# Layer 0's attention heads of images 1 to 3 written as one sequence with the bias computed five blocks ahead

## The chip, the cores and the metric

The kernel runs on one core of a Trainium2 chip. The metric is the device time of one execution in microseconds. The core has five engines with a queue each: TensorE (PE in the profile; its weight loads are PEld), VectorE (DVE), ScalarE (ACT), GpSimd (POOL) and SyncE (SP, which here issues DMAs). Each queue holds a fixed list of instructions and works it in order; an instruction that waits holds up everything behind it in its own queue. Matmul results go to PSUM, of which the kernel has two tiles of two banks ("big") and four of one bank ("bank").

## The reference, cut to what matters

Four layers follow each other on a batch of four images of 32 x 32 positions and 384 channels, each with a residual sum. The change is in the first, a deformable attention with 6 heads of 64 channels. Of it, what the changed code computes:

```python
attn = jnp.einsum('bmhc,bnhc->bhmn', qh, k) * scale
disp = (ref.reshape(1, n, 1, 2) - pos.reshape(Bq * G, 1, n, 2)) * 0.5
...
bias = _bilinear_sample(rpe_img, disp)          # one position table for each head
...
attn = jax.nn.softmax(attn + bias, axis=-1)
out = jnp.einsum('bhmn,bnhc->bmhc', attn, v).reshape(Bq, Hq, Wq, NC)
```

For each head, 1024 queries attend to 1024 sampled keys. To each logit a bias is added that is sampled bilinearly from a table, at a place that depends on the key's sampled position and on the query.

## The kernel before, in words

All data is float32. The program has two lanes of work. The front is layer 0 of an image; the trunk is layers 1 to 3 of an image. Image 0's front runs almost alone (`heads0`, ordered by hand, untouched by the change). After that, `Net.layer3` steps through the trunk of image b and, between its steps, through the front of image b+1: each generator yields the weight of the work it has just written, and the front is kept 0.1 of an image ahead. So the program text of trunk and front is interleaved. A planner then orders each engine's queue at build time: an instruction written earlier has the better rank, one that is not ready in the planner's reckoning is passed by one that is, and tiles of a tag share a fixed number of buffers. An edge without a semaphore (`add_manual_dep` with class NoSync) only forces one instruction behind another in a queue.

The heads of images 1 to 3 are written in `Front.layer0`: for each head h and each half q of the queries (16 rows, 512 queries) it calls `head0(h, q)`, a half-head; there are 12 of them in an image. Keys lie on the partitions, in eight blocks j of 128; queries lie on the free axis. A half-head does:

- **Bias and logits**, for each block: a gather by GpSimd (L830) fetches for each key a window of 17 rows of the table into `win` (4 buffers); ScalarE scales the upper rows into `z` (L842; 3 buffers) and VectorE adds the lower rows times their weight (L843); ScalarE scales the left columns into `lg` (L847; 13 buffers) and VectorE adds the right columns (L848). These four are one block's bias steps. Then TensorE multiplies keys and queries (L851), VectorE adds the product to the bias (L852) and keeps the running maximum over the blocks in `rmax` (L855, L857).
- **Maximum chain**: TensorE transposes `rmax` (L864), VectorE reduces it to one maximum for each query (`top`, L868), GpSimd puts the maxima on a diagonal (`diag`, L870), TensorE multiplies that with ones (L872), so that every partition has every query's maximum, and ScalarE copies it out of PSUM (`tb`, L876).
- **Softmax and values**, for each block: VectorE subtracts `tb` (L883), ScalarE takes the exponential (L884), TensorE accumulates values (`va`) and sums (`ones`) into one PSUM tile `po` (L886). At the end ScalarE copies the values over the queries in `qpad` (L890) and the sums into a row of the first `lg` tile (L893), and SP sends that row to `den` in DRAM (L894).

After every second head, `over_sums(k)` (L1112 to L1132) fetches the sums of two heads, inverts them (L1118), sends them to `rden` (L1121), loads them back, spread over the partitions, into two tiles of the tag `lg` (L1126) and multiplies `qpad` with them (L1131). `load_keys(h)` (SP) puts head h's keys into one of two padded tiles `kz`, one head ahead.

In the trunk, the longest stretch that runs beside the heads is layer 1's `pair`: TensorE's L1514, L1544, L1539, L1486 and L1381, ScalarE's exponentials L1522 and L1390 and its copies L1556, VectorE's L1551, L1389, L1477, L1480 and (at a pair's start) L1445, GpSimd's L1497 (`sg`).

## Time and profile before

| | us |
|---|---|
| median of 3 runs | 4557.96 (4557.15 to 4560.0) |
| the profiled execution | 4561.78 |
| its span, first to last instruction | 4560.0 |
| mean granted TensorE clock | 0.943 |

The profile is of one execution. Its page gives busy times of each engine, the granted TensorE clock (1.00 is full speed), and groups of instructions by source line, each with the idle time of the engine just before it and what ended that idle time (the releaser). Some groups on the changed lines, from the same profile:

| line | engine, what | count | mean ns |
|---|---|---|---|
| L830 | GpSimd, gather of `win` | 288 | 1122 |
| L842 / L847 | ScalarE, bias rows / columns | 288 each | 736 / 717 |
| L843 / L848 | VectorE, bias rows / columns | 288 each | 763 / 777 |
| L852 / L857 | VectorE, logit sum / running maximum | 288 / 216 | 684 / 688 |
| L868 | VectorE, reduction to `top` | 36 | 690 |
| L870 | GpSimd, diagonal | 36 | 1165 |
| L876 | ScalarE, copy to `tb` | 36 | 584 |
| L883 / L884 | VectorE subtraction / ScalarE exponential | 288 each | 701 / 628 |

The busy time of TensorE can hide slack, since its matmuls are pipelined and their ends are modelled; its idle time and the granted clock can be read off more surely.

### The profile page before, as it was taken

How to read it: one execution, taken by the hardware profiler on the slowest of the kernel's cores; microseconds unless marked ns; L12 is line 12 of the kernel's file. 1: busy time of each engine (PE TensorE's matmuls, PEld its weight loads, DVE VectorE, ACT ScalarE, POOL GpSimd, SP SyncE). 2: the span in 40 equal slices, each digit the busy share in tenths (PEclk: the TensorE clock that was granted, in tenths of full speed). 3: DMA queues.
4: the chain of work that ended last, by engine and by line, in shares of the span. 5: the costliest groups of instructions: out<-in, count | busy, mean ns of one | idle time of the engine just before them, and what ended most of it. 6: DMA issues, size and time to landing. Idle time of an engine off the chain costs nothing.

```text
span 4560.0 us, 47383 instructions
## 1 busy us (share of the span) xinstructions
PE 4131.4 (91%) x15896; PEld 1776.3 (39%) x15896; DVE 3135.2 (69%) x5909; ACT 2302.7 (50%) x3633; POOL 970.7 (21%) x978
## 2 busy tenths in 40 slices
PE   5699889999999898999999989799999998999998
PEld 2333334333334453433333444343333335344444
DVE  4599456878887627678878753667787874566654
ACT  2266334666664313556766332356566641466632
POOL 1644123212121103311212010422121211000000
PEclk8799899999999888999999989899999998999998
DMA  6444234222221244422322124532122213311011
GB/s 140 150 143 131 74 115 127 83 55 73 60 63 58 81 117 137 115 57 55 85 55 77 41 87 121 164 94 60 39 79 55 77 38 114 120 29 37 23 40 42
DMA packets 235924, 377.30 MB, mean 83 GB/s; under 512 B 117763, under 2 KB 167264, under 8 KB 235680
## 3 DMA queue, kind: packets, MB, share of 16 engines
q1 hardware_dynamic: 183640, 207.55, 16.2%
q0 software_dynamic: 39936, 145.53, 11.0%
q10 hardware_dynamic: 12104, 21.19, 1.4%
q8 instruction: 126, 2.06, 0.2%
q14 instruction: 118, 0.97, 0.1%
HBM read 294.19 MB, written 80.27 MB: 82 GB/s over the span
## 4 chain that ended last, share of the span: by engine, by line
PE 56%; DVE 15%; issue 7%; ACT 6%; DMA 3%; POOL 1%; another core or an unknown queue 0%; SPq 0%; ACTq 0%; DVEq 0%; POOLq 0%
PE bank L1544 13%; PE big L1514 5%; PE big L403 4%; PE bank L886 4%; PE bank L417 4%; PE big L1381 4%; PE bank L851 4%; PE bank L1486 3%; PE bank L1539 3%; DVE nmax L1389 2%; ACT big L1390 2%; PE bank L1219 2%; DVE e L1551 2%; PE big L666 2%; PE big L1684 1%
## 5 line engine op out<-in xcount | busy, mean ns | idle before, releaser
L1544 PE MATMUL bank<-whole,sg 128*128 128x512 f32 (+3 forms) x2304 | 847.0, 501 | 2.6 <-POOL sg L1497 2.6
L1551 DVE SCALAR_TENSOR_TENSOR e<-bank,gam,e 128x512 f32<-128x512 f32 x768 | 560.7, 748 | 316.2 <-PE bank L1544 177.3
L1390 ACT ACTIVATE big<-big,nmax 128x1024 f32<-128x1024 f32 x384 | 417.7, 1088 | 283.3 <-DVE nmax L1389 262.2
L1522 ACT ACTIVATE e<-big 128x1024 f32<-128x1024 f32 x384 | 381.1, 1020 | 328.2 <-PE big L1514 321.2
L1544 PEld LDWEIGHTS bank<-whole,sg 128*128 128x128 f32 x2304 | 399.4, 196 | 351.5 <-issue 259.4
L1389 DVE TENSOR_REDUCE nmax<-big 128x1 f32<-128x1024 f32 x384 | 453.2, 1219 | 84.6 <-PE big L1381 53.5
L830 POOL DMA_INDIRECT win<-strips,widx x288 | 323.2, 1122 | 703.3 <-DVE z L843 350.7
L1514 PE MATMUL big<-qa,ka 64*128 64x512 f32 x1536 | 432.8, 643 | 24.6 <-ACT big L1390 23.6
L1497 POOL TENSOR_SCALAR sg<-whole,gam 128x512 f32<-128x512 f32 x192 | 145.9, 760 | 1327.0 <-PE bank L1544 1064.5
L1381 PE MATMUL big<-k,q 32*128 32x512 f32 x1536 | 287.9, 662 | 43.2 <-ACT big L1390 26.0
L738 POOL DMA_INDIRECT gat<-pairs,sidx x192 | 206.2, 1074 | 412.9 <-DVE ix_gt L519 227.4
L851 PE MATMUL bank<-qpad,kz 128*128 128x512 f32 x576 | 280.6, 616 | 8.9 <-ACT gn L1556 8.3
L886 PE MATMUL bank<-lg,va 128*64 128x512 f32 x576 | 267.7, 609 | 21.4 <-ACT lg L884 21.3
L886 PE MATMUL bank<-lg,ones 128*64 128x512 f32 x576 | 267.0, 609 | 0.0
L848 DVE SCALAR_TENSOR_TENSOR lg<-z,bias_f,lg 128x512 f32<-128x512 f32 x288 | 220.0, 777 | 58.3 <-ACT lg L847 55.4
L1514 PEld LDWEIGHTS big<-qa,ka 64*128 64x128 f32 x1536 | 138.4, 190 | 280.1 <-issue 125.5
L1486 PE MATMUL bank<-e,vs 128*32 128x512 f32 x1536 | 231.1, 620 | 8.6 <-DVE vs L1480 8.4
L842 ACT ACTIVATE z<-win,bias_f 128x528 f32<-128x528 f32 x288 | 204.1, 736 | 42.2 <-DVE lg L848 22.2
L843 DVE SCALAR_TENSOR_TENSOR z<-win,bias_f,z 128x528 f32<-128x528 f32 x288 | 214.5, 763 | 8.5 <-issue 4.3
L883 DVE TENSOR_TENSOR lg<-lg,tb 128x512 f32<-128x512 f32 x288 | 187.0, 701 | 47.6 <-ACT tb L876 47.6
L852 DVE TENSOR_TENSOR lg<-bank,lg 128x512 f32<-128x512 f32 x288 | 192.2, 684 | 31.3 <-PE bank L851 30.6
L847 ACT ACTIVATE lg<-z,bias_f 128x512 f32<-128x512 f32 x288 | 201.5, 717 | 13.4 <-PE bank L886 5.7
(312 smaller groups left out, 6582.8 us busy)
## 6 DMA issues: line engine op xcount, KB each, us to landing
pairs<-xn SPq DMA_DIRECT2D x64, 192.0 KB
q<-qd SPq DMA_DIRECT2D x48, 256.0 KB
xg<-xgd SPq DMA_DIRECT2D x48, 256.0 KB
w<-in_gmat SPq DMA_DIRECT2D x16, 576.0 KB
w<-in_w_off SPq DMA_DIRECT2D x12, 576.0 KB
w<-in_Wqkv SPq DMA_DIRECT2D x12, 576.0 KB
a<-in_x SPq DMA_DIRECT2D x16, 384.0 KB
x<-a ACTq DMA_DIRECT2D x4, 1536.0 KB
```

The costliest lines, as they stand in the source:

```text
L830: nc.gpsimd.indirect_dma_start(out=win, out_offset=None, in_=self.strips[:, :], in_offset=bass.IndirectOffsetOnAxis(ap=self.widx[:, q, c : ...
L848: v.scalar_tensor_tensor(lg, z[:, :, 1 : HW + 1], sc(0, 0), lg, ALU.mult, ALU.add)
L851: nc.tensor.matmul(ps, kz[:, j * P : (j + 1) * P], both, start=True, stop=True)
L886: nc.tensor.matmul(po[out, :], w, lf, start=j == 0, stop=j == NJ - 1)
L1381: nc.tensor.matmul(ps[r][:, h * 512 : (h + 1) * 512], self.q4[rows, i * P : (i + 1) * P], self.k4[rows, 0:512], start=True, stop=True,)
L1389: v.tensor_reduce(nmax[:, r, i : i + 1], ps[r], AX.X, ALU.max, negate=True)
L1390: nc.scalar.activation(ps[r], ps[r], AF.Exp, bias=nmax[:, r, i : i + 1], accum_out=den[:, r, i : i + 1],)
L1486: nc.tensor.matmul(av[r0 : r0 + HD1, :], vs[:, r, :], es[h][:, r, :], start=j == 0, stop=j == NJ - 1,)
L1514: nc.tensor.matmul(ps[:, r, :], ka[rows, j * P : (j + 1) * P], qa[rows, cols], start=True, stop=True,)
L1522: nc.scalar.activation(e, ps, AF.Exp)
L1544: last = nc.tensor.matmul(ps[:, (mid - i0) * P :], sg[:, r, m, :], sim[:, h, r, m, (mid - i0) * P :], start=m == 0, stop=m == 1,)
L1551: v.scalar_tensor_tensor(e[:, r, :], ps, self.gam[:, 1:2], e[:, r, :], ALU.add, ALU.mult, accum_out=tot[:, r, h : h + 1],)
```

## The change

`head0` is gone; `Front.layer0` calls one generator `heads1` for the whole image. It numbers the 96 blocks (head, half, block) in one sequence. A call `bias()` writes the row steps of the next block and the column steps of the one before it; the row steps first issue the gather of the block two further on. Five calls stand ahead of the first logit. Each half-head then has eight more: after the logits of blocks 1, 3 and 5, between the transposes and the reduction to `top`, between the ones-matmul and the copy to `tb`, and after the softmax of blocks 1, 4 and 7. So at the start of each half-head the bias of its first five blocks is written already, across heads and across `over_sums`. `chain` puts an edge without a semaphore from each head instruction on VectorE, and likewise on ScalarE, to the one written before it on that engine (the two copies at the end of a half-head, `over_sums` and the trunk are outside). The sums now go out of PSUM into a row of `tb`. The yields are split anew (2.5 for each logit block, 2 after the reduction, 2 after the copy, 1.375 for each softmax block, 3 at the end); their sum for a half-head stays 38. The numbers of buffers stay.

```diff
             with self.scope("l0b"):
-                self.load_keys(0)
-                for h in range(G):
-                    if h + 1 < G:
-                        self.load_keys(h + 1)
-                    for q in range(2):
-                        yield from self.head0(h, q)
-                    if h % 2:
-                        yield from self.over_sums(h // 2)
+                yield from self.heads1()
...
+        def chain(ins):
+            engine = ins.ins.engine
+            if engine in last:
+                self.tc.add_manual_dep(
+                    ins.ins,
+                    last[engine],
+                    mybir.DependencyInfo(
+                        mybir.DependencyClass.NoSync, mybir.DependencyReason.DATA
+                    ),
+                )
+            last[engine] = ins.ins.name
...
+        def rows_of(i):
+            gather(i + 2)
+            if i < n:
+                wv = win.pop(i).rearrange("p (r c) -> p r c", c=WROW)
+                z[i] = self.wt([P, HH, HW + 1], "z", 3)
+                chain(nc.scalar.activation(
+                    z[i], wv[:, 0:HH, 0 : HW + 1], AF.Copy, scale=sc(i, 1, 1)
+                ))
+                chain(v.scalar_tensor_tensor(
+                    z[i], wv[:, 1 : HH + 1, 0 : HW + 1], sc(i, 1, 0), z[i], ALU.mult, ALU.add
+                ))
+
+        def cols_of(i):
+            if i < n:
+                zi = z.pop(i)
+                lg[i] = self.wt([P, HN], "lg", 13)
+                out = lg[i].rearrange("p (y x) -> p y x", x=HW)
+                chain(nc.scalar.activation(out, zi[:, :, 0:HW], AF.Copy, scale=sc(i, 0, 1)))
+                chain(v.scalar_tensor_tensor(
+                    out, zi[:, :, 1 : HW + 1], sc(i, 0, 0), out, ALU.mult, ALU.add
+                ))
+
+        todo = iter(range(n))
+
+        def bias():
+            i = next(todo, n)
+            rows_of(i + 1)
+            cols_of(i)
+
+        self.load_keys(0)
+        gather(0)
+        gather(1)
+        rows_of(0)
+        for _ in range(5):
+            bias()
+        for h in range(G):
+            if h + 1 < G:
+                self.load_keys(h + 1)
...
+            for q in range(2):
+                first = (2 * h + q) * NJ
...
+                for j in range(NJ):
+                    lf = lg[first + j]
+                    ps = self.bank()
+                    nc.tensor.matmul(
+                        ps, self.kz[h % 2][:, j * P : (j + 1) * P], both, start=True, stop=True
+                    )
+                    chain(v.tensor_tensor(lf, ps, lf, ALU.add))
+                    if j:
+                        chain(v.tensor_tensor(rmax, lg[first] if j == 1 else rmax, lf, ALU.max))
+                    if j % 2 and j < 6:
+                        bias()
+                    yield 2.5
+
+                ps = self.bank()
+                for i in range(NI):
+                    nc.tensor.transpose(
+                        ps[:, i * P : (i + 1) * P], rmax[:, i * P : (i + 1) * P], self.ident
+                    )
+                top = self.wt([P, NI], "top", 2)
+                bias()
+                chain(v.tensor_reduce(top, ps.rearrange("p (i n) -> p i n", i=NI), AX.X, ALU.max))
                 yield 2
...
+                tb = self.wt([P, HN], "tb", 2)
+                bias()
+                chain(nc.scalar.copy(tb, ps))
+                yield 2
+
+                po = self.bank()
+                for j in range(NJ):
+                    lf = lg.pop(first + j)
+                    chain(v.tensor_tensor(lf, lf, tb, ALU.subtract))
+                    chain(nc.scalar.activation(lf, lf, AF.Exp))
...
+                    if j % 3 == 1:
+                        bias()
+                    yield 1.375
...
+                den = tb[o0 : o0 + 1, :]
+                nc.scalar.copy(den, po[o0 : o0 + 1, :])
+                nc.sync.dma_start(self.den[h][:, q * HN : (q + 1) * HN], den)
+                yield 3
+            if h % 2:
+                yield from self.over_sums(h // 2)
```

## The prediction

> **What bounds the kernel.** I read the page's busy shares first, then its chain of waits, then the stretches in which the heads of images 1 to 3 run.
>
> ```profile
> span 4560.0 us, 47383 instructions
> PE 4131.4 (91%) x15896; PEld 1776.3 (39%) x15896; DVE 3135.2 (69%) x5909; ACT 2302.7 (50%) x3633; POOL 970.7 (21%) x978
> PE 56%; DVE 15%; issue 7%; ACT 6%; DMA 3%; POOL 1%; another core or an unknown queue 0%; SPq 0%; ACTq 0%; DVEq 0%; POOLq 0%
> L886 PE MATMUL bank<-lg,va 128*64 128x512 f32 x576 | 267.7, 609 | 21.4 <-ACT lg L884 21.3
> ```
>
> TensorE is the bound and the change takes no matmul away, so it can only win or lose TensorE's idle time and what goes with it, the granted clock. The heads' queue order matters where they run: by the starts of L842 and L886, 785 to 1560, 1905 to 2660 and 3018 to 3765 us. The busy time by stretch (columns: stretch, its length, busy PE, PEld, DVE, ACT, POOL, granted clock, DMA share, GB/s):
>
> ```profile
> 1270.30:1325.10 54.80, 54.64 (x232) 21.78 (x232) 39.32 (x79) 29.64 (x51) 3.82 (x5) 1.00 0.07 16
> 1325.10:1387.70 62.60, 56.35 (x211) 22.87 (x207) 59.21 (x121) 50.15 (x78) 27.32 (x24) 0.92 0.39 116
> 1079.70:1151.20 71.50, 63.11 (x228) 23.46 (x229) 67.34 (x122) 54.95 (x88) 28.20 (x26) 0.93 0.41 116
> 833.60:1509.80 676.20, 635.41 (x2526) 254.26 (x2526) 543.07 (x1060) 407.81 (x645) 128.66 (x129) 0.97 0.22 60
> 1949.30:2625.80 676.50, 636.16 (x2525) 255.09 (x2525) 542.35 (x1059) 407.89 (x645) 129.01 (x129) 0.97 0.21 60
> 3062.50:3739.00 676.50, 637.17 (x2526) 255.45 (x2526) 542.31 (x1059) 407.74 (x645) 128.29 (x129) 0.97 0.21 60
> ```
>
> The last three rows are one image's heads each, from the first logit sum (L852) to the last. TensorE idles 40.8, 40.3 and 39.3 us there (length less PE), 120.5 in all. The first row is one half-head with TensorE idle for 0.2 us; the second is the next, with 6.3 us idle, VectorE full (59.2 of 62.6) and the clock at 0.92. So the idle time is bunched. Why there? VectorE and ScalarE shortly before the third row, and SP's queue:
>
> ```profile
> 1068.82 0.75 DVE L1551 SCALAR_TENSOR_TENSOR e<-bank,gam,e 128x512 f32<-128x512 f32 x1 [5.33 <-PE bank L1539]
> 1074.10 2.51 SPq L1126 DMA_DIRECT2D lg<-rden  x4
> 1076.62 1.32 ACT L847 ACTIVATE lg<-z,bias_f 128x512 f32<-128x512 f32 x2
> ```
>
> Half-head 4 of each image (counting from 0) comes after an `over_sums`, which takes two of the 13 `lg` buffers for its reciprocals. No L847 of half 4 runs until those two transfers (L1126) issue at 1074.10; all eight start after 1076. VectorE had stood idle 5.33 us shortly before, then does all eight biases together with the eight logit sums. Half 8, after the second `over_sums`, does the same (its first L847 starts at 1323, after the loads at 1320). I read this as buffers given out in the order of the program text: half 4's `lg` tiles stand behind the two reciprocals. Counting L843 against L883 by eights, the other halves mostly run far ahead: in 21 of 36 half-heads the next half's eight L843 have started before the first subtraction.
>
> **The change, term by term,** against the profiled run's own 4561.8 us (span 4560.0 and 1.8 around it). Instruction counts per image stay: 96 gathers, 192 bias steps on each of ScalarE and VectorE, the same matmuls and key loads. The sum of exponents is copied into `tb` and not the first `lg`: the same 577 ns L893 and the same DMA, so nothing; it frees an `lg` buffer earlier.
>
> *1. The refill after over_sums.* In the new text five blocks of half 4 (and of half 8) stand ahead of `over_sums`, so their `lg` tiles no longer queue behind the reciprocals, and their bias falls where VectorE stood idle. The six bunched stretches of the three images are 71.5, 62.6, 70.8, 60.7, 72.6 and 62.7 us long, with PE idle 8.4, 6.3, 6.6, 8.0, 6.6, 6.8: 42.6 us. Their clocks are 0.93, 0.92, 0.93, 0.94, 0.88, 0.92; (1 - clock) x length, the time that full clock would have saved, is 5.0 + 5.0 + 5.0 + 3.6 + 8.7 + 5.0 = 32.3 us. Together 74.9. They won't become perfect: the other 30 half-heads have 120.5 - 42.6 = 77.9 us idle and, at 0.97 over 2029 us (60.9), 28.6 us lost to the clock, 3.5 us each. Gain: 74.9 - 6 x 3.5 = 54. Bounds: 0 (the three biases left in the logits fill VectorE all the same) to 75.
>
> *2. Bias calls inside the maximum chain.* One stands between the transposes (L864) and the reduction (L868), one between the ones-matmul (L872) and the copy (L876). In the first, VectorE does two steps of 763 and 777 ns; in a row they start 0.67 us apart (as L1551 at 1082.13 and 1082.80), so 1.34 us against the 0.75 us for which L868 waits now: it comes 0.6 us later. In the second, ScalarE does 736 + 717 = 1453 ns while the diagonal (1165) and its matmul (1130) take 2.3 us: hidden; if a trunk exponential (1020) gets between them, 0.2 late. What is late next is the exponential and its matmul L886. TensorE feels it only where it stands uncovered: L864, L872 and L886 idled 17.9 + 13.5 + 21.4 = 52.8 us over the run, and a fully uncovered chain costs 0.86 + 0.85 + 2.06 = 3.77 (half 0 of image 1), so 14 chains' worth of 36. 14 x 0.6 = 8, with the second call up to 14 x 0.8 = 11: I take 10. Lower bound 0; the upper is the rival D below.
>
> *3. Smoothing elsewhere.* After the tops of halves 1 and 5 VectorE is 90% busy (23.66 of 26.2 us, 23.77 of 26.3) doing a burst of biases with the subtractions, and TensorE idles 3.2 and 2.0 us: 15.6 us over three images. With three biases per softmax at fixed places I take half: -8. Bounds -16 and 0.
>
> *4. Less done ahead at the start of an image.* Before, 13 biases of halves 0 and 1 are done before the first sum; now five. Eight more, 8 x 1.34 = 10.7 us of VectorE, move into half 0, where VectorE was idle 7.1 and 7.6 us (two stretches of 27.6 and 40.0 us): hidden, 0. If that room is gone, +32 over three images.
>
> *5. The queues passed.* Each bias call issues a gather on POOL, two blocks ahead; one now stands just before the diagonal in that queue. Its 1122 ns run while VectorE does the two steps and the reduction (2.0 us), and POOL is 21% busy: 0. If it issues late, the diagonal and a trunk sg L1497 behind it wait up to 1.1 us, +15 over the 14 uncovered chains. SP's queue: key loads and den are where they were. The accumulator holds its bank longer, since the exponentials are spread; nearest row is L851's 8.3 us on gn L1556: 0 to +8, I take 0.
>
> *6. The chains themselves* add no semaphore on their own engine. They make a head step that isn't ready hold the head steps behind it, on both engines; the trunk's steps can still be placed between, so I count nothing here beyond term 2.
>
> Sum: -54 + 10 - 8 = -52, so 4510 for the profiled run; the median lies 3.8 under it: **4506 us**.
>
> The Trainium skill, page "TensorE: Matmul & The Clock Gate", section "Why this matters for your kernels", asks only for no TensorE gaps above about 3 us. The trace shows 0.93 in the third row above, whose longest gap is 2.12 us (1103.25 to 1105.37, for L1480), so short bunched gaps cost clock here too. By the page the clock would not be part of the gain: 42.6 - 6 x 2.6 = 27 in term 1, and 4533.
>
> **Rivals.**
> A, the forecast, 4475 to 4545, 44%.
> B, more of the bound comes back: bias spread evenly also takes half of what the other 30 half-heads lose (30 x 3.5 / 2 = 52): 4454, 14%. For it: VectorE is 80% busy on average (543 of 676), so an even load leaves slack everywhere. Against: much of that idle time is the trunk's own waits (L1381 on L1522, L1420 on L1413).
> C, the bunch only moves: `over_sums` gets its reciprocals at the same time and the sixth bias tile still queues behind them, in order on VectorE, holding the sums. Term 1 is 0: 4558, within 0.2%, 8%.
> D, slower: the maximum chain stands uncovered in every half-head. At half 3 its wait is hidden (0.2 us idle) because the trunk has matmuls ready and VectorE has nothing else. Now VectorE and ScalarE have bias work in order at both of its waits, nothing can be done further ahead than five blocks, and the gap becomes 3.77 + 0.6 = 4.37 us, 36 times: 157 instead of 53, +104. With terms 1 and 3: 4610. It turns the result slower once about 12 of the 22 covered chains lose their cover (52 / 4.37). 34%. For it: in half 0 the chain leaves VectorE and TensorE idle together even without bias calls. Against: trunk steps stand between the reduction and the copy in the new text.
>
> **Numbers.** About 0.2% (9 us) can be told from no change. Faster is A and B, 0.58; same 0.08; slower 0.34. The range 4440 to 4620 holds A, C, D and most of B, and leaves out an outcome above D (two mishaps of term 4 and 5's size) and one below B.
>
> **What would show it.** Right: in half-heads 4 and 8, bias steps (ScalarE lg from z) before the reciprocals' loads, VectorE below 90% and the clock near 1.00; PE idle in an image's heads down from 40 to about 28 us. Term 2: the reduction starting 0.6 us later after the transposes. Wrong: the waits of the transposes, the ones-matmul and the value matmuls summing to well over 53 us (D), or idle time and clock in the heads as before (C).

## The result, and the profile after

The changed kernel takes **4610.14 us** (median of 4 runs, 4609.27 to 4612.8) where the kernel before took 4558.98 (4557.15 to 4560.25) on the same chip: a ratio of 1.0112, 95% interval [1.0099, 1.0124]. It is 51 us slower; the prediction said 4506. Chips differ by up to 27 us for the kernel before, so every ratio below is to the kernel before on the same chip.

The page of the changed kernel: the span, the busy shares, the chain that ended last, and two of its groups (line, engine, operation, tiles, count, busy us, mean ns, idle us before and what ended it).

```profile
span 4611.0 us, 47251 instructions
PE 4139.6 (90%) x15896; PEld 1766.4 (38%) x15896; DVE 3158.0 (68%) x5909; ACT 2305.4 (50%) x3633; POOL 969.1 (21%) x978
PE 53%; DVE 20%; ACT 7%; issue 5%; DMA 3%; POOL 1%; SPq 0%; another core or an unknown queue 0%; ACTq 0%; POOLq 0%; DVEq 0%
L936 PE MATMUL bank<-lg,va 128*64 128x512 f32 x576 | 300.8, 652 | 53.4 <-ACT lg L931 53.2
L867 ACT ACTIVATE lg<-z,bias_f 128x512 f32<-128x512 f32 x288 | 206.5, 717 | 219.9 <-DVE z L857 219.6
```

TensorE's busy time grew by 8 us (4131.4 to 4139.6), the span by 51: 43 us of the loss are idle time. VectorE's share of the last chain rose from 15 to 20%. The value matmul (L936, before L886) waits 53.4 us for exponentials instead of 21.4, and ScalarE's column step (L867, before L847) stood idle 219.9 us for VectorE's row step, where it was 13.4 before.

The same stretches as in the prediction, of the changed kernel (stretch, its length, busy time of the five engines, granted clock, DMA share, GB/s). The first six rows are half-heads 8 and 4 of the first image and 4 and 8 of the other two, each from its first logit sum (now L900) to that of the next half-head; the last three are one image's heads each, from the first logit sum to the last.

```profile
1338.80:1401.20 62.40, 54.43 (x216) 22.99 (x215) 45.14 (x96) 36.83 (x57) 14.40 (x13) 0.95 0.21 58
1083.90:1152.30 68.40, 59.16 (x244) 22.50 (x244) 53.92 (x104) 43.31 (x68) 13.07 (x13) 0.95 0.28 75
2210.70:2278.80 68.10, 59.44 (x244) 23.29 (x244) 54.16 (x105) 43.38 (x68) 13.07 (x13) 0.95 0.28 76
2465.20:2526.30 61.10, 53.91 (x216) 21.96 (x216) 45.11 (x97) 36.90 (x57) 14.58 (x13) 0.97 0.21 61
3336.60:3405.30 68.70, 59.27 (x244) 22.69 (x244) 54.04 (x104) 43.35 (x68) 13.06 (x13) 0.95 0.27 74
3591.70:3652.70 61.00, 53.87 (x216) 21.96 (x215) 44.99 (x97) 36.84 (x57) 14.40 (x13) 0.97 0.20 59
831.00:1529.60 698.60, 638.70 (x2522) 250.97 (x2522) 562.93 (x1078) 418.54 (x660) 139.06 (x139) 0.97 0.22 62
1958.70:2657.10 698.40, 640.28 (x2519) 252.69 (x2519) 562.68 (x1077) 417.30 (x659) 138.41 (x139) 0.97 0.22 62
3083.80:3783.50 699.70, 640.87 (x2519) 252.16 (x2519) 562.60 (x1077) 417.50 (x659) 138.22 (x139) 0.97 0.22 62
```

Idle time of TensorE in the three images (length less PE): 59.9 + 58.1 + 58.8 = 176.8 us, against 120.5: 56 us more. The granted clock is 0.97 as before to two digits; the time at half clock in these stretches, summed from the trace, is 126.3 us, before 112.6. In half-heads 4 and 8 the load did what the change says: in the first two rows VectorE is at 72% (45.14 of 62.40) and 79% (53.92 of 68.40) instead of 95 and 94% (59.21 of 62.60, 67.34 of 71.50). TensorE idles no less for it: 8.0 and 9.2 us, before 6.3 and 8.4. Over the six rows its idle time is 49.6 us, before 42.6; (1 - clock) x length is 17 us, before 32; their lengths sum to 389.7 us, before 400.9. So the half-heads that the prediction was about became 11 us shorter, and the whole loss lies in the others.

The groups of TensorE that wait more, from the list of groups by line:

```profile
L919 PE MATMUL bank<-diag,ones 128*128 128x512 f32 x72 | 41.9, 665 | 41.0 <-POOL diag L917 41.0
L909 PE MATMUL bank<-ident,rmax 128*128 128x128 f32 x144 | 23.0, 282 | 18.0 <-DVE rmax L902 18.0
L1592 PE MATMUL bank<-ident,gn 128*128 128x128 f32 x576 | 120.6, 292 | 23.4 <-DVE lg L900 16.3 <-DVE e L1604 5.7 <-DVE lg L868 1.0
```

The maximum chain's three waits (L909, L919, L936; before L864, L872, L886) went from 17.9 + 13.5 + 21.4 = 52.8 to 18.0 + 41.0 + 53.4 = 112.4 us. The trunk's transposes L1592 (before L1539) now wait for a bank that the logit sum L900 frees (16.3). Summed from the trace over the three images' stretches (waits above 0.15 us), the heads' own matmuls (logits, transposes, diagonal, values) wait 114.9 us, before 56.8. The trunk's waits there only changed places: those of L1381, L1420, L1486 and L1514 of before and their successors fell from 48.3 to 14.5 us, those of its L1539 and L1659 rose from 13.9 to 41.4, and in all they are 60.0 us, before 62.2. So the 56 us are the heads' own waits, those of the maximum chain. Outside these stretches TensorE idles 14 us less.

Where each half-head's time goes, by the mean over the 36 half-heads, worked out from the trace (us):

| from, to | before | after |
|---|---|---|
| transposes end, reduction to `top` starts | 0.17 | 0.64 |
| reduction ends, diagonal starts on GpSimd | 0.11 | 0.42 |
| transposes end, first subtraction starts | 4.67 | 5.32 |
| first subtraction starts, eighth ends | 7.63 | 14.30 |

The last row is the largest change: the eight subtractions, 0.7 us each, are now spread over twice the time, and the exponentials and value matmuls with them.

### The profile page after: what moved, and what is told of

It is laid out like the page before. It is cut to its first block, busy times and chain, and to the rows that moved or that the text cites. A ratio compares the mean times of both kernels' runs of the same rounds, so it can differ in the third digit from the quotient of the medians.

```text
span 4611.0 us, 47251 instructions
## 1 busy us (share of the span) xinstructions
PE 4139.6 (90%) x15896; PEld 1766.4 (38%) x15896; DVE 3158.0 (68%) x5909; ACT 2305.4 (50%) x3633; POOL 969.1 (21%) x978
## 4 chain that ended last, share of the span: by engine, by line
PE 53%; DVE 20%; ACT 7%; issue 5%; DMA 3%; POOL 1%; SPq 0%; another core or an unknown queue 0%; ACTq 0%; POOLq 0%; DVEq 0%
PE bank L1597 12%; PE big L1567 5%; PE bank L936 4%; PE big L403 4%; PE bank L417 4%; PE big L1434 4%; PE bank L897 3%; PE bank L1592 3%; DVE nmax L1442 2%; PE bank L1539 2%; DVE e L1604 2%; DVE lg L900 2%; DVE lg L868 2%; PE big L659 2%; DVE rmax L902 2%
## 5 line engine op out<-in xcount | busy, mean ns | idle before, releaser
L1604 DVE SCALAR_TENSOR_TENSOR e<-bank,gam,e 128x512 f32<-128x512 f32 x768 | 559.0, 747 | 334.1 <-PE bank L1597 225.0
L1442 DVE TENSOR_REDUCE nmax<-big 128x1 f32<-128x1024 f32 x384 | 452.8, 1218 | 67.6 <-PE big L1434 52.9
L1567 PE MATMUL big<-qa,ka 64*128 64x512 f32 x1536 | 415.7, 630 | 12.1 <-ACT big L1443 11.2
L936 PE MATMUL bank<-lg,va 128*64 128x512 f32 x576 | 300.8, 652 | 53.4 <-ACT lg L931 53.2
L867 ACT ACTIVATE lg<-z,bias_f 128x512 f32<-128x512 f32 x288 | 206.5, 717 | 219.9 <-DVE z L857 219.6
L1434 PE MATMUL big<-k,q 32*128 32x512 f32 x1536 | 276.0, 652 | 27.6 <-ACT big L1443 18.0
L936 PE MATMUL bank<-lg,ones 128*64 128x512 f32 x576 | 300.8, 652 | 0.0
L857 DVE SCALAR_TENSOR_TENSOR z<-win,bias_f,z 128x528 f32<-128x528 f32 x288 | 219.7, 763 | 84.5 <-ACT z L854 77.2
L868 DVE SCALAR_TENSOR_TENSOR lg<-z,bias_f,lg 128x512 f32<-128x512 f32 x288 | 241.1, 837 | 2.7 <-ACT lg L867 2.3
L931 ACT ACTIVATE lg<-lg 128x512 f32<-128x512 f32 x288 | 176.5, 629 | 123.5 <-DVE lg L930 119.1
L1539 PE MATMUL bank<-e,vs 128*32 128x512 f32 x1536 | 229.2, 606 | 0.0
L900 DVE TENSOR_TENSOR lg<-bank,lg 128x512 f32<-128x512 f32 x288 | 196.3, 685 | 41.6 <-PE bank L897 41.2
```

The costliest lines, as they stand in the source:

```text
L868: chain(v.scalar_tensor_tensor(out, zi[:, :, 1 : HW + 1], sc(i, 0, 0), out, ALU.mult, ALU.add))
L936: nc.tensor.matmul(po[out, :], w, lf, start=j == 0, stop=j == NJ - 1)
L1434: nc.tensor.matmul(ps[r][:, h * 512 : (h + 1) * 512], self.q4[rows, i * P : (i + 1) * P], self.k4[rows, 0:512], start=True, stop=True,)
L1442: v.tensor_reduce(nmax[:, r, i : i + 1], ps[r], AX.X, ALU.max, negate=True)
L1539: nc.tensor.matmul(av[r0 : r0 + HD1, :], vs[:, r, :], es[h][:, r, :], start=j == 0, stop=j == NJ - 1,)
L1567: nc.tensor.matmul(ps[:, r, :], ka[rows, j * P : (j + 1) * P], qa[rows, cols], start=True, stop=True,)
```

## The experiments

The change has three parts that can be taken apart: the **sequence** (the bias steps written five blocks ahead, at their new places in the text), the **edges** on VectorE and on ScalarE, and the **yields** (how the trunk's text is dealt into a half-head). The edges and the places come first, then the yields, then the edges again.

### Edges taken away, new yields kept

All edges away, in the changed kernel:

```diff
-            if engine in last:
+            if False:
```

> The changed kernel without the edges that chain the head steps on VectorE and ScalarE; places, lead and yields stay. Theory M (the maximum chain: bias calls written ahead of the reduction and of the copy to tb keep it waiting, and TensorE idles 112 us on transposes, ones-matmul and value matmuls instead of 53): the bias calls keep their better rank, so 4600 or more. Theory R (the rigid order itself): back to 4560 or below, with the three waits near 53 us.

Measured: 1.0127 [1.0107, 1.0147]. Without edges it is as slow as with them, so the edges alone don't explain the result under these yields.

Edges on VectorE alone:

```diff
-            if engine in last:
+            if engine in last and engine == mybir.EngineType.DVE:
```

> The changed kernel with the edges on VectorE alone; ScalarE's head steps are free. ScalarE idles 220 us in the changed kernel on columns that wait for VectorE's row step. Theory M: ScalarE is 50% busy and not what TensorE waits for: 4605 to 4615. Theory R in its ScalarE form (a queued column step that waits holds back exponentials): down by 20 or more, and the value matmuls' wait on the exponential falls below 35 us.

Measured: 1.0043 [1.0029, 1.0058]. Against the changed kernel's 1.0112, which was timed on another chip, ScalarE's edges cost 0.7%, but taking VectorE's away too gives it back. Something else was in play.

### The two bias calls in the maximum chain

Each of the two calls moved behind the instruction that it stood before:

```diff
-                bias()
                 chain(v.tensor_reduce(top, ...))
+                bias()
...
-                bias()
                 chain(nc.scalar.copy(tb, ps))
+                bias()
```

> The changed kernel with two of the bias calls moved one step later: the one before the reduction to top now stands behind it, the one before the copy to tb behind that copy. Theory M: the ones-matmul's wait falls from 41 us to about 14 and the value matmuls' from 53 to about 40; 4610 goes down by some 40 to 4570. Theory R (edges) and theory L (only five blocks of lead, less work-ahead to fill VectorE): within 10 us of 4610.

Measured: 1.0220 [1.0201, 1.0240]. The expectation had the wrong sign. The trace says why, in the value matmul's group:

```profile
L936 PE MATMUL bank<-lg,va 128*64 128x512 f32 x576 | 307.6, 665 | 101.0 <-ACT lg L931 100.5
```

101.0 us instead of 53.4: the bias steps on VectorE now stand between the copy and the first subtraction, which starts 2.05 us after the copy's end (mean of 36; 0.27 in the changed kernel). The wait only moved one link on.

No calls in the chain at all, but at logit blocks 0, 2, 4, 6 and softmax blocks 4 to 7; first with both chains of edges, then with VectorE's alone:

```diff
-                    if j % 2 and j < 6:
+                    if j % 2 == 0:
                         bias()
...
-                bias()
                 chain(v.tensor_reduce(top, ...))
...
-                bias()
                 chain(nc.scalar.copy(tb, ps))
...
-                    if j % 3 == 1:
+                    if j > 3:
                         bias()
```

> The changed kernel with no bias call between the last logit and the first softmax step: calls behind logits 0, 2, 4, 6 and behind softmax steps 4 to 7; edges on both engines stay. Theory M (bias steps queued inside the maximum chain keep it waiting): the subtraction follows the running maximum within 7 us as in the kernel before, the waits of transposes, ones-matmul and value matmuls sum to 60 us or less instead of 112, and the ratio to the kernel before falls from 1.011 to 1.005 or lower. Theory R (edges on ScalarE): 1.008 or more. Theory P (any rewriting of the text loses about 1% because the planner's order before was a good draw): 1.005 to 1.015 whatever the waits do.

> The same places as the run before it in this list, with the edges on VectorE alone. If M and the ScalarE edges each cost their part (1.0112 down to 1.0043 without the ScalarE edges), both gone give 0.995 to 1.000. If only the ScalarE edges matter: 1.003 to 1.006. If P: 1.005 to 1.015.

Measured: 1.0243 [1.0211, 1.0275] and 1.0078 [1.0061, 1.0095]. Both are worse than with the calls in the chain (1.0112 and 1.0043), and on one chip the two differ by 1.7%, which is what ScalarE's edges cost at these places. The first subtraction did come closer to the transposes' end (4.81 and 4.78 us, from 5.32 and 5.44), but the stretch of the eight subtractions grew from 14.30 to 17.31, and from 10.97 to 13.31. Of the two calls taken out of the chain one went to the logits and one to the softmax, whose four calls now follow each other in its second half; there they cost more.

### The refill alone, and the sums in `tb`

The kernel before with `over_sums` written one half-head later, so that the next half-head's `lg` tiles no longer stand behind the reciprocals:

```diff
                     for q in range(2):
                         yield from self.head0(h, q)
-                    if h % 2:
-                        yield from self.over_sums(h // 2)
+                        if q == 0 and h in (2, 4):
+                            yield from self.over_sums(h // 2 - 1)
+                yield from self.over_sums(2)
```

> The kernel before, with over_sums written one half-head later (behind the first half of the next head), so that its two lg tiles no longer stand ahead of the next half-head's biases. This is term 1 of the prediction by itself. Theory T1: half-heads 4 and 8 fill ahead like the others, VectorE below 90% there, 4559 goes down by about 54 to 4505. Rival: the bunch moves on to the next half-head, or the trunk's pair start sets those stretches anyway: 4550 to 4565.

Measured: 1.0094 [1.0074, 1.0113]. The refill that my largest term was about is worth nothing by itself; this way of getting it costs 0.9%. In its trace at least eight blocks of bias are done at the first logit sum of every half-head (2 and 1 at half-heads 4 and 8 of the kernel before), and still VectorE is 90 to 95% busy from there to the last logit sum of half-heads 4 and 8: the steps done earlier make room for those of the next half-head, which fill it. The six stretches idle 48.4 us, before 42.6; the rest of the loss lies in the other half-heads (107.9 us idle, before 77.9), and why is open. What happens to the waits in half-head 4 when VectorE has room can be seen in TensorE's timelines of the kernels before and after (start, us, engine, line, tiles, count, idle time before and its releaser; the longest waits there). Before:

```profile
1105.37 1.89 PE L1486 MATMUL bank<-e,vs 128*32 128x512 f32 x8 [2.12 <-DVE vs L1480]
1110.66 1.13 PE L872 MATMUL bank<-diag,ones 128*128 128x512 f32 x2 [0.99 <-POOL diag L870]
1121.22 3.08 PE L1381 MATMUL big<-k,q 32*128 32x512 f32 x8 [1.30 <-ACT big L1390]
1145.25 3.21 PE L1381 MATMUL big<-k,q 32*128 32x512 f32 x8 [1.78 <-ACT big L1390]
```

After:

```profile
1111.75 0.66 PE L909 MATMUL bank<-ident,rmax 128*128 128x128 f32 x4 [1.23 <-DVE rmax L902]
1115.27 1.91 PE L919 MATMUL bank<-diag,ones 128*128 128x512 f32 x2 [1.81 <-POOL diag L917]
1119.24 1.12 PE L936 MATMUL bank<-lg,va 128*64 128x512 f32 x1 [2.06 <-ACT lg L931]
```

Before, 5.2 of the 8.4 us (the first, third and fourth line) are the trunk's waits for its own softmax, while VectorE is full. After, VectorE has room and these waits are gone, but the head's maximum chain waits in their place, 5.1 us of the 9.2.

The kernel before with the sums copied into a row of `tb`:

```diff
-        den = logits[0][o0 : o0 + 1, :]
+        den = tb[o0 : o0 + 1, :]
```

> The kernel before with the sums of exponentials copied into a row of tb and not of the first lg tile, the change's smallest part alone. The prediction put it at nothing: 0.998 to 1.002. Theory P (a small edit re-draws the planner's order): outside of that, most likely above.

Measured: 0.9994 [0.9983, 1.0004]. Nothing, as costed.

### The yields

The kernel before with nothing but the new yields:

```diff
-            yield 3
+            yield 2.5
...
         v.tensor_reduce(top, ps.rearrange("p (i n) -> p i n", i=NI), AX.X, ALU.max)
+        yield 2
...
         nc.scalar.copy(tb, ps)
-        yield 3
+        yield 2
...
-            if j % 2:
-                yield 2
+            yield 1.375
```

> The kernel before with the new split of the yields alone (2.5 for each logit block, 2 after the reduction, 2 after the copy, 1.375 for each softmax block): the same instructions, the trunk's text only interleaved differently. Theory M: the yields are not what costs, 0.998 to 1.003. Theory P: 1.004 to 1.012, as much as the change itself.

Measured: 1.0124 [1.0107, 1.0141]: the yields alone cost as much as the whole change. The split of the chain's yield by itself, then the shift from logits to softmax by itself:

```diff
         v.tensor_reduce(top, ps.rearrange("p (i n) -> p i n", i=NI), AX.X, ALU.max)
+        yield 2
...
         nc.scalar.copy(tb, ps)
-        yield 3
+        yield 1
```

> The kernel before with one part of the new yields: the 3 after the tb copy becomes 2 after the reduction and 1 after the copy, so that trunk text stands between the reduction and the diagonal; the sum stays 38. Theory Ya (trunk steps dealt into the maximum chain delay it): 1.005 to 1.012, the idle time of the diagonal's and value matmuls up by 15 us or more. Theory Yb (it is the shift of trunk text from logits to softmax): 1.000 within 0.003.

```diff
-            yield 3
+            yield 2.5
...
             if j % 2:
-                yield 2
+                yield 3
```

> The kernel before with the other part: 2.5 in place of 3 after each logit block, 3 in place of 2 after every second softmax block; the sum stays 38. Theory Yb (trunk text moved from logits to softmax makes the exponentials late and the value matmuls wait): 1.005 to 1.012, L886 idle from 21 to about 40 us. Theory Ya: 1.000 within 0.003. If both parts cost about half, or each about 1 percent, it is not one place but any re-dealing of the order (theory P).

Measured: 0.9994 [0.9981, 1.0008] and 1.0118 [1.0098, 1.0137]. It is the shift. Half-head 3 of the first image (counting from 0) shows what it does, by TensorE's timeline from the ones-matmul to the first value matmuls. Before:

```profile
1051.43 1.12 PE L872 MATMUL bank<-diag,ones 128*128 128x512 f32 x2
1052.39 1.04 PE L1539 MATMUL bank<-ident,gf 128*128 128x128 f32 x8
1053.27 1.95 PE L1544 MATMUL bank<-whole,sg 128*128 128x512 f32 x4
1055.15 1.14 PE L1381 MATMUL big<-k,q 32*128 32x512 f32 x8
1056.22 1.98 PE L1544 MATMUL bank<-whole,sg 128*128 128x512 f32 x4
1058.13 1.06 PE L1486 MATMUL bank<-e,vs 128*32 128x512 f32 x6
1059.12 0.64 PE L886 MATMUL bank<-lg,va 128*64 128x512 f32 x1
```

With the shift:

```profile
1047.58 1.12 PE L872 MATMUL bank<-diag,ones 128*128 128x512 f32 x2 [0.85 <-POOL diag L870]
1048.63 1.13 PE L1514 MATMUL big<-qa,ka 64*128 64x512 f32 x4
1049.69 1.04 PE L1486 MATMUL bank<-e,vs 128*32 128x512 f32 x2
1050.77 0.64 PE L886 MATMUL bank<-lg,va 128*64 128x512 f32 x1
...
1052.20 0.64 PE L886 MATMUL bank<-lg,va 128*64 128x512 f32 x1 [0.35 <-ACT lg L884]
```

Before, 6.7 us of trunk work (1052.39 to 1059.12) lie over the copy, the subtractions and the exponentials, and the value matmuls then run without a wait. With the shift only 2.1 us lie there, and the diagonal's matmul waits as well. Over the run the three waits of the chain go from 10.4 to 23.0 us in the odd half-heads, which were covered before, and from 42.4 to 50.4 in the even ones. Why less trunk text falls there, though the yield behind the copy is 3 in both, no run takes apart. The idle time is half of the loss: 147.2 us in the images' heads, before 120.5. The other half is TensorE's busy time, 4152.4 us, before 4131.4; it rose in the value matmuls (L886 with `va` 283.7 us, before 267.7) and the logits' (L851 287.5, before 280.6), whose busy time can hide slack.

Does any re-dealing cost, then? The shift the other way, and more trunk text right behind the copy, twice:

```diff
-            yield 3
+            yield 3.25
...
             if j % 2:
-                yield 2
+                yield 1.5
```

> The kernel before with the shift the other way: 3.25 in place of 3 after each logit block, 1.5 in place of 2 after every second softmax block, sum 38 as before. Theory P (the order before is a good draw and every re-dealing loses about 1 percent): 1.008 to 1.014. Theory C (only taking trunk work away from the logits costs, since the chain then stands uncovered in every half-head): 0.995 to 1.003.

```diff
         nc.scalar.copy(tb, ps)
-        yield 3
+        yield 5
...
             if j % 2:
-                yield 2
+                yield 1.5
```

> The kernel before with 5 in place of 3 after the copy to tb and 1.5 in place of 2 after every second softmax block: more trunk text right behind the maximum chain. Theory C: the chain is better covered, the idle time of the transposes', diagonal's and value matmuls falls from 53 us, 0.990 to 0.999. Theory P: 1.008 to 1.014.

```diff
         nc.scalar.copy(tb, ps)
-        yield 3
+        yield 7
...
             if j % 2:
-                yield 2
+                yield 1
```

> The kernel before with 7 in place of 3 after the copy to tb and 1 in place of 2 after every second softmax block, sum 38. 5 gave 0.9984 [0.9969, 0.9999]. If cover over the chain is what is short: 0.993 to 0.998. If the chain was already covered in the odd half-heads and the even ones can't be reached this way: 0.998 to 1.001; if the softmax is starved of trunk work instead: above 1.002.

Measured: 1.0003 [0.9989, 1.0016], 0.9984 [0.9969, 0.9999] and 0.9983 [0.9972, 0.9994]. So a new order does not cost by itself. Of the dealings tried, those that cost take trunk work away from the stretch before the first value matmul. The first of the three also warns against reading one wait alone: its diagonal's matmul waits 37.4 us, before 13.5, but the value matmuls' wait (21.4 to 10.2) and the trunk's in the heads (62.2 to 45.9) fell by as much together. The other two are the only small gains of the study, some 8 us each, ahead of both kernels; in the last the value matmuls wait 15.4 us instead of 21.4. Their intervals lie below 1, though the gain is no larger than the 0.2% that the prediction named as what can be told.

### The sequence under the old yields

The yields of before put back into the changed kernel (3, none, 3, 2 after every second softmax block), with both chains of edges:

```diff
-                    yield 2.5
+                    yield 3
...
                 chain(v.tensor_reduce(top, ...))
-                yield 2
...
                 chain(nc.scalar.copy(tb, ps))
-                yield 2
+                yield 3
...
-                    yield 1.375
+                    if j % 2:
+                        yield 2
```

> The changed kernel with the old yields (3 after each logit block, none between reduction and diagonal, 3 after the tb copy, 2 after every second softmax block); sequence, bias places and both chains of edges stay. Theory Y (the whole loss is how the trunk's text is dealt into a half-head; sequence and edges together give nothing): 1.000, within 0.003, and the waits of the diagonal's and the value matmuls back to about 35 us in sum, as in the kernel before. Theory S (the sequence with its edges costs by itself, and the two losses don't add): 1.008 to 1.014. Theory S+ (they add): above 1.014, which would mean the changed yields had helped here.

With VectorE's edges alone, besides those yields:

```diff
-            if engine in last:
+            if engine in last and engine == mybir.EngineType.DVE:
```

> The same with edges on VectorE only. The edges on ScalarE cost 0.7 and 1.7 percent in two pairs so far. Y: 0.990 to 0.998, faster than the kernel before, the expectation of the forecast's gain at last; S: 1.000 to 1.006. If it equals the run with both edges, the cost of ScalarE's edges depends on the new yields.

Without edges, besides those yields:

```diff
-            if engine in last:
+            if engine in last and False:
```

> The changed kernel with the old yields and without edges. Theory E (the edges cost by themselves, the sequence does not): 0.997 to 1.003, idle time in the heads back near 120 us, against 1.0126 with edges. Theory T (the place of the bias steps in the program text costs, whether or not edges hold them): 1.008 to 1.014.

With VectorE's edges, those yields and no bias calls in the chain (calls at logit blocks 0, 2, 4, 6 and softmax blocks 4 to 7, as in the earlier pair):

```diff
-                bias()
                 chain(v.tensor_reduce(top, ...))
...
-                bias()
                 chain(nc.scalar.copy(tb, ps))
```

> Old yields, edges on VectorE only, bias calls at logit blocks 0, 2, 4, 6 and softmax blocks 4 to 7, none between reduction and tb. TensorE's order is then that of the kernel before to within some per cent. Theory M (under the old order the bias steps inside the chain uncover it: reduction to first subtraction 4.1 and 5.3 us against 3.6 and 4.9): 1.000 to 1.004, below the 1.0077 of the same with calls in the chain. Theory N (five blocks ahead at fixed places load the softmax and the logits whatever the places): 1.007 or more.

Measured: both 1.0126 [1.0098, 1.0153]; VectorE's alone 1.0077 [1.0051, 1.0104]; none **1.0039** [1.0026, 1.0051]; VectorE's alone and no calls in the chain 1.0106 [1.0078, 1.0134]. The sequence by itself costs 0.4%, VectorE's edges another 0.4, ScalarE's another 0.5; the intervals of neighbours touch, so the 0.9% from none to both is surer than its parts. Calls outside the chain are no better here either (the two intervals overlap). Here are the two kernels that differ in nothing but the edges (value matmul L935, diagonal's matmul L918, column step L867). Without:

```profile
L935 PE MATMUL bank<-lg,va 128*64 128x512 f32 x576 | 267.1, 608 | 21.4 <-ACT lg L930 21.3
L918 PE MATMUL bank<-diag,ones 128*128 128x512 f32 x72 | 42.4, 672 | 16.0 <-POOL diag L916 16.0
L867 ACT ACTIVATE lg<-z,bias_f 128x512 f32<-128x512 f32 x288 | 205.8, 718 | 21.3 <-DVE z L857 13.9 <-PE bank L935 5.3 <-issue 1.2
```

With:

```profile
L935 PE MATMUL bank<-lg,va 128*64 128x512 f32 x576 | 300.0, 660 | 62.3 <-ACT lg L930 62.1
L918 PE MATMUL bank<-diag,ones 128*128 128x512 f32 x72 | 46.2, 727 | 45.2 <-POOL diag L916 45.1
L867 ACT ACTIVATE lg<-z,bias_f 128x512 f32<-128x512 f32 x288 | 206.8, 718 | 215.6 <-DVE z L857 208.7 <-DMA whole<-x 6.5
```

How the edges do it stands in VectorE's timeline of half-head 3 (L914 reduction, L929 subtractions, L1442 the trunk's maximum, L857 and L868 VectorE's two steps of the bias call written behind the second subtraction; the trunk's L1604 left out). Without edges:

```profile
1005.23 0.76 DVE L857 SCALAR_TENSOR_TENSOR z<-win,bias_f,z 128x528 f32<-128x528 f32 x1
1006.91 0.75 DVE L868 SCALAR_TENSOR_TENSOR lg<-z,bias_f,lg 128x512 f32<-128x512 f32 x1 [0.92 <-ACT lg L867]
...
1051.44 0.69 DVE L914 TENSOR_REDUCE top<-bank 128x4 f32<-128x512 f32 x1 [0.81 <-PE bank L909]
...
1056.38 1.29 DVE L929 TENSOR_TENSOR lg<-lg,tb 128x512 f32<-128x512 f32 x2
...
1058.26 1.90 DVE L929 TENSOR_TENSOR lg<-lg,tb 128x512 f32<-128x512 f32 x3
1060.06 2.35 DVE L1442 TENSOR_REDUCE nmax<-big 128x1 f32<-128x1024 f32 x2
```

With edges:

```profile
1047.58 0.68 DVE L914 TENSOR_REDUCE top<-bank 128x4 f32<-128x512 f32 x1
...
1052.85 1.28 DVE L929 TENSOR_TENSOR lg<-lg,tb 128x512 f32<-128x512 f32 x2
...
1055.46 0.77 DVE L857 SCALAR_TENSOR_TENSOR z<-win,bias_f,z 128x528 f32<-128x528 f32 x1 [0.66 <-ACT z L854]
1056.14 2.35 DVE L1442 TENSOR_REDUCE nmax<-big 128x1 f32<-128x1024 f32 x2
1058.41 0.74 DVE L868 SCALAR_TENSOR_TENSOR lg<-z,bias_f,lg 128x512 f32<-128x512 f32 x1
...
1059.74 1.89 DVE L929 TENSOR_TENSOR lg<-lg,tb 128x512 f32<-128x512 f32 x3
```

The third subtraction starts 6.82 us after the reduction without edges and 12.16 with them. A bias call is four steps: ScalarE row, VectorE row, ScalarE column, VectorE column; the column steps belong to the block before, so they do not wait for the row steps of the same call. Both chains hold them in text order, so the third subtraction stands behind the call's column step on VectorE, that behind its row step, and that waits for ScalarE's row step, which stands behind the second exponential. Between VectorE's two steps the planner fits in the trunk's 2.35 us reductions, and the subtraction is later still. Without edges the same call's steps had run some 50 us earlier, and only trunk steps stand between the subtractions.

At last, whether cover behind the copy helps where the edges stand (the edit is against the first kernel of this section, with both chains):

```diff
                 chain(nc.scalar.copy(tb, ps))
-                yield 3
+                yield 5
...
                     if j % 2:
-                        yield 2
+                        yield 1.5
```

> The changed kernel (sequence, bias calls in the chain, both edges) with 3 after each logit block, none between reduction and diagonal, 5 after the copy to tb and 1.5 after every second softmax block. The same with 3 and 2 gave 1.0126 and 57.5 us idle at the value matmuls. If the uncovered chain carries the loss: 1.002 to 1.008, that idle time below 40 us. If it only stands beside it: 1.010 to 1.014.

Measured: 1.0120 [1.0100, 1.0141], and the value matmuls still wait 59.2 us (62.3 in that kernel). Cover in front of the first value matmul does nothing when the exponentials come late all through the softmax.

### The runs side by side

Ratio to the kernel before, and in brackets the mean stretch of the eight subtractions in us (7.6 in the kernel before):

| | old yields | new yields |
|---|---|---|
| text of before | 1 (7.6) | 1.0124 (5.8) |
| sequence, no edges | 1.0039 (7.6) | 1.0127 (5.8) |
| edges on VectorE | 1.0077 (11.3) | 1.0043 (11.0) |
| edges on both | 1.0126 (14.2) | 1.0112 (14.3), the change |

Four of these runs (no edges and VectorE's edges under the new yields, the calls behind the chain, the sums later) were timed on a chip where the kernel before takes 4533.78 us, 20 us less than on any other; they compare best among themselves.

The edges also do some good. With them exactly five blocks of bias are done at the first logit sum of nearly every half-head; without them it is 5 to 13, and 5 or 6 at half-heads 4 and 8. That levels VectorE: over half-heads 4 and 8 it is 77 to 81% busy with both chains and 86 to 90% without edges (old yields). The trunk's two largest waits in the heads' stretches (L1381 and L1420 of before and their successors) are 36 us before, 47 with the sequence and no edges, and 8 with both chains of edges (old yields). Other waits of the trunk, of its transposes above all, take part of that back, so that all its waits there are 62.2 us before, 65.5 and 49.8; and the chain's waits take more than the rest.

There are two causes of the loss, and they don't add. The yields put the value matmuls too early: the subtractions come quickly, but no trunk work covers them. The edges draw the softmax out. That a drawn-out softmax takes in the trunk work that the new yields deal into it would fit the lower rows; no run shows that by itself. Open is also why TensorE's busy time rises by 22 us with the new yields on the kernel before (4131.4 to 4153.1), with the same matmuls; the value matmuls hold most of it (L887 with `va` 287.7 us, before 267.7).

## Why the prediction was wrong

**The bound** was read rightly: TensorE does the same 15896 matmuls, its busy time moved by 8 us and its idle time by 43.

**Term 1, the refill (-54), failed.** The refill alone gave +0.9%, not -1.2%, and the sequence without edges, which also does its bias across `over_sums`, +0.4%. In the changed kernel VectorE's bunch was levelled as described (without edges only to 84 to 90%), but the six stretches became 11 us shorter and not 54. Of their 32 us of lost clock 15 came back. Their idle time, which was to fall from 42.6 to 15.6 us (6 x 2.6), is 49.6: the trunk's waits for its softmax are gone, and waits of the head's maximum chain stand there instead. I had treated the idle time of a stretch as gone with its cause, and had not asked what would be waited for next.

**Term 2, the calls in the chain (+10), had the right delay and the wrong count.** The reduction came 0.47 us later on the mean (0.6 foreseen), the diagonal another 0.31 on GpSimd. But it met far more than 14 chains: the value matmuls wait in 33 of the 36 half-heads (15 before), the diagonal's in 30 (19 before). At most that is 36 x 0.65 us (the end of the transposes to the first subtraction), 23 us. Still, no other place tried for these calls was better.

**Term 3 (-8)**: from the first subtraction to the next half-head's first logit sum, half-heads 1 and 5 idle 1.9 us each, before 3.2 and 2.0: half of the gain counted. From the transposes on it is 3.6 and 2.7 us, where the chain had cost nothing before, so in sum nothing was won. **Term 4 (0)** held: the first half-head of an image idles 6.8 us, before 6.6. **Term 5 (0)**: GpSimd's queue was passed at 0.31 us a chain, as above; the accumulator cost nothing (the logits matmul's wait went from 8.9 to 4.0).

**Term 6, the chains of edges ("I count nothing here"), is the step that failed on the losing side.** Under the old yields they cost 0.9%, some 40 us; under the new ones, whose own loss is as large, taking them away changes nothing (1.0127). I had looked at whether the trunk's steps could pass; what mattered was that bias steps could no longer run ahead of the softmax, and that each call between two subtractions makes the second wait for an exponential and a step on the other engine. The eight subtractions take 14.3 us instead of 7.6.

**The yields had no term at all.** I wrote their new numbers down and noted the same sum, and used them once, as an argument against rival D ("trunk steps stand between the reduction and the copy in the new text"). Alone they cost 1.2%.

**Rival D** had the direction and the place: the chain stands uncovered in nearly every half-head. It had it from the bias calls, where edges and yields do it. Its price was too high: the three waits came to 112.4 / 36 = 3.1 us a half-head, not 4.37, so +60 and not +104. That its 4610 is the time measured is chance. By its own terms it is 4561.8 + 104 - 54 - 8 - 3.8 = 4600, since the 104 stand in place of term 2's 10 and do not come on top of them; and the gains of terms 1 and 3 that it kept came only to 11 us and to nothing.

**The clock.** The prediction counted 32 us of lost clock in the bunched stretches and set the Trainium skill's rule beside it (page "TensorE: Matmul & The Clock Gate", section "Why this matters for your kernels": no gaps above about 3 us). In these stretches 15 of the 32 us came back (some 5 may be scatter: the kernel with the sums in `tb` has 27 there). That it came from levelling VectorE is not shown: with no calls in the chain and both chains of edges VectorE is at 68 to 72% there, and 29 us are lost. The other half-heads lost more. With 56 us more idle time in the images' heads, their time at half clock rose from 112.6 to 126.3 us, though the longest gap in them is 2.89 us. By that rule alone these gaps would have cost no clock; here they went with more of it lost.

## What to carry to other kernels

Before counting a stretch's idle time as a gain, ask which wait stands there once its cause is gone, and what covers that one now. Forcing an order on two in-order engines is not free even without semaphores: a step that goes from one to the other, placed between two steps of a softmax, puts its passage in front of the second, where a free order had run it long before. Where two programs are dealt into one another, the weights that deal them are part of the schedule; a change of them is costed like any other, by the work that lies over each wait.

## What the runs showed of the hardware

The clock falls to half although no gap is long. TensorE's clock in the changed kernel around the chain of half-head 4 (columns as above):

```profile
1110.00:1115.50 5.50, 2.46 (x13) 0.95 (x10) 5.46 (x8) 2.87 (x4) 2.20 (x3) 1.00 0.58 139
1115.50:1122.30 6.80, 4.74 (x10) 0.88 (x9) 3.41 (x6) 3.06 (x5) 1.94 (x2) 0.50 0.22 73
```

In the first row TensorE was busy 2.46 of 5.50 us, with gaps of 1.23 and 1.81 us; then the clock was 0.50 for 6.8 us, in the middle of the value matmuls. So a few short gaps close together can do it. The kernel before has the like in its half-head 4:

```profile
1100.00:1105.50 5.50, 3.38 (x14) 1.07 (x16) 5.50 (x13) 4.08 (x6) 2.51 (x2) 1.00 0.63 167
1105.50:1108.90 3.40, 3.40 (x13) 1.24 (x10) 2.32 (x4) 1.60 (x3) 0.95 (x1) 0.50 0.34 79
```

TensorE was busy for 3.38 of 5.50 us, with one gap of 2.12, and then 3.40 us at 0.50, all of them busy. Over the 20 kernels profiled here, idle time of TensorE and time at half clock in the images' heads rise together (correlation 0.84), from 107 and 68 us in the last of the three re-dealings above to 228 and 143 us with the bias calls behind the chain. The Trainium skill's page on TensorE, in its section "A second HAM failure mode: psum-queue depth-cycling", tells of another kernel in which frequent short idle times made the clock swing; these rows agree with that section, and not with a limit of about 3 us for one gap.
